# A slot's gathers, a finished tile's root and two exponentials put at other places in the second step of a top-p graph layer

## The chip, the core and the metric

The kernel runs on one core of one Trainium2 chip. A time is the device time of one execution in microseconds. The core has five engines that work side by side, each through its own list of instructions in order: PE (matmuls and transposes), ACT (activation functions and copies out of PSUM), DVE (passes over rows, maxima), POOL (small arithmetic, and the gathers, whose addresses it works out) and SP (which only issues transfers). They wait for one another by semaphores.

## The reference

A graph of N = 3327 nodes with 256 features each. After a layer norm with ReLU, two steps are made; in each, an attention over all nodes is cut to the largest probabilities that make up 0.9 of a row (top-p), and the sparse adjacency matrix spreads the features.

```python
def _top_p_attention(X, W1, W2, W3):
    q = X @ W1.T @ W2.T
    k = X @ W3.T
    probs = jax.nn.softmax(q @ k.T / TAU, axis=-1)
    idx = jnp.argsort(-probs, axis=-1)
    sp = jnp.take_along_axis(probs, idx, axis=-1)
    keep_sorted = jnp.cumsum(sp, axis=-1) - sp < TOP_P
    ...
    A = probs * mask
    return A / jnp.maximum(A.sum(-1, keepdims=True), 1e-12)
...
for n in range(STEPS):
    A = _top_p_attention(Xa, W1, W2, W3)
    Xf = R @ Xf
    Xa = A @ Xa
    Z = Z + Xf @ U1[n].T + Xa @ U2[n].T
h = X + Z
...
x = x + layernorm(h)
```

R is the adjacency plus the identity, each row divided by its sum.

## The kernel before

The nodes stand in 26 tiles of 128 rows. For each tile a row of 3328 exponentials `e` is made, and the top-p threshold of each row is found without sorting: it is guessed from a law of the row's moments, the guess is measured with a few passes over `e`, and then the exact threshold is settled among the candidates just below the guess. The second step runs in slots, one per tile, and a slot holds work of several tiles at once, each at another stage. A slot has seven parts (k = 0 to 6). What stands in a part, and in which order, is written out by hand: `PLAN[1]` has a string per part, and each letter lets one piece of work go one yield further. The lists of PE, ACT, DVE and POOL keep exactly this order (an in-order dependency is put between each two neighbours). Slots -1 to 3 and 25 to 27 have strings of their own (`OPEN`, `LAST`); `PLAN[1]` rules slots 4 to 24.

The letters of slot i, with the lines that matter here:

- `m`, the guess for tile i+1 (`measured_twice`). In k=0 ACT works out the first guess (up to L676) and POOL prepares columns of `g` (L677, L678, L679). In k=1 and 3 ACT makes two passes over `e` (L634). In k=4 DVE takes their sums (L686, L687), ACT a logarithm and an exponential (L688, L689), POOL four operations (L690 to L693). In k=5 comes a third pass (L634). In k=6 DVE, ACT and POOL make the second guess of it (DVE L700, L701, L707, L708; ACT L703 to L705; POOL L698, L699, L709 to L713). `n` in the next slot's k=1 is its last exponential on ACT (L715).
- `d` and `c`, settling tile i (`settle`) on DVE: the pass L730 makes `w`, the values below the guess (k=2); 20 MAX8 (L735) take the best of each segment; L742 and L744 sort out the best 40; the pass L764 masks `e` with the threshold (`c`, next slot's k=0).
- `w`, the exponentials of tile i+2: four quarters, each of matmuls (L601) and an exponential on ACT (L605; the last one L609 and L611); two in k=2, one in k=4, one in k=6. `q` makes the queries of tile i+3 (L524, L529).
- `g`, the gathers of tile i+2 (`refetch`, `fetched`): POOL issues five indirect transfers of 128 rows (L922) into one of two buffers `xg`. Together with the first, SP is asked for the packed adjacency (`ac` from `cx`).
- `s`, the sparse product of tile i from its gathered rows: six matmuls (L930), the result added on DVE (L1120).
- `f`, finishing tile i-2: DVE adds the attention's sum (L954) and takes the statistics (L459, L460); POOL makes the root (L466, L467, L962: the reciprocal standard deviation and its product with the mean); in the next slot's k=2 POOL scales the tile (L969 to L972) and SP sends it out.

Between the letters PE transposes `e` in seven groups (L810), ACT copies each out (L812), and PE multiplies them with the features (L824). In L679, `g`'s column 3 is read, into which L686 writes the next value of that column:

```python
G.tensor_scalar(col(7), col(3), ms(3), ms(8), ALU.mult, ALU.add)
...
V.tensor_scalar(col(3), oa[:, 1:2], float(NP), col(9), ALU.add, ALU.mult)
```

Of the kernel before, what the change touches and what calls it, by code (L numbers as in the profile page):

```python
# [345 lines left out]
def guess_graph_layer(ctx, tc, x, adj, w1t, w2t, w3t, u1t, u2t, ln_g, ln_b, out, flag):  # L346
# [780 lines left out]
    def refetch(t):  # L1127
# [7 lines left out]


    PLAN = (("gmdsssa", "gmcdsssa", "edawwpg", "gmsdga", "gmspdea", "ohgdawwqg", "gehmgq"),
            ("llcmss", "lnms", "lwwnfd", "lcmdsssgggg", "fdsmwqdf", "llmdf", "lmwdg"))

    LAST = {NT - 1: ("cfss", "cn", "nd", "sss", "fddddddsf", "f", ""), NT: ("c", "", "", "ff", "ff", "fv", "f"),  # L1140
            NT + 1: ("fv", "f", "", "", "f", "f", "f")}
# [98 lines left out]
@with_exitstack  # L1240
def tile_graph_layer(ctx, tc, *args):
    keep = ctx.enter_context(tc.tile_pool(name="keep", bufs=1))
    flag = keep.tile([1, 1], I32, tag="flag", name="flag")
    guess_graph_layer(tc, *args, flag)
    failed = tc.nc.values_load(flag[0:1, 0:1], min_val=0, max_val=1 << 20)
    with tc.If(failed > 0):
        search_graph_layer(tc, *args)
# [34 lines left out]
```

## Time and profile before

| | |
|---|---|
| median of three runs | 1345.82 us (1345.72 to 1351.75) |
| the profiled execution | 1354.65 us, its span 1352.9 us |
| second step, from L730 of tile 0 to the end of the span | 771.10 to 1352.9 us |
| busy over the span: PE, DVE, ACT, POOL | 1269.8, 1164.4, 1082.9, 1019.6 us |
| granted TensorE clock over the span | 0.985; 1.00 in all windows from 830 to 1280 us |

Rows of a timeline give start, duration (both in us), engine, line, operation, the tile written and those read, shapes, and how many instructions the row stands for; in brackets stands how long the engine was idle just before, and what ended that. Rows of windows give the stretch, its length, then the busy time of PE, of PE's weight loads, of DVE, ACT and POOL with the number of instructions, and then the granted clock, the transfers' share and GB/s. Matmuls' ends are modelled, and spans on POOL are rough.

### The profile page before, as it was taken

The page shows a single profiled execution, that of the slowest core. Times are in us where ns is not written, and L with a number is a line of the kernel's source. Part 1 is how long each engine was busy: PE and PEld are TensorE (multiplying, and loading weights), DVE is VectorE, ACT ScalarE, POOL GpSimd, SP SyncE. Part 2 cuts the span into 40 slices and gives each one's busy share as a digit, 9 for nine tenths or more (in the row PEclk, how much of TensorE's full clock was granted, in tenths as well). Part 3 has the DMA queues.
Part 4 walks back from the last instruction along what each step waited for, and adds up shares of the span by engine and source line. Part 5 has one row for each costly group of instructions (what it writes and reads, how often), then busy time and mean ns, then how long its engine had stood idle before and what let it go on. Part 6 is the DMA issues. An engine that isn't in the chain of part 4 may idle for free.

```text
span 1352.9 us, 22127 instructions
## 1 busy us (share of the span) xinstructions
PE 1269.8 (94%) x6495; PEld 976.5 (72%) x6495; DVE 1164.4 (86%) x3481; ACT 1082.9 (80%) x2368; POOL 1019.6 (75%) x1405
## 2 busy tenths in 40 slices
PE   5989999999999999999999579999999999999985
PEld 4635777878777777777777457777777777777774
DVE  5867799999999999999890689899898989989893
ACT  4385788888888879888763789999998999999951
POOL 5114788888888888887883577888888888888862
PEclk9999999999999999999999879999999999999998
DMA  8634545454454544545443212221212222131200
GB/s 276 205 127 131 146 137 159 125 151 146 136 158 124 160 139 137 157 133 152 125 111 88 73 53 68 74 90 51 91 56 86 64 82 87 54 90 51 91 24 23
DMA packets 92642, 149.77 MB, mean 111 GB/s; under 512 B 15425, under 2 KB 59072, under 8 KB 92512
## 3 DMA queue, kind: packets, MB, share of 16 engines
q1 hardware_dynamic: 75056, 105.37, 24.5%
q0 software_dynamic: 16640, 42.69, 12.4%
q8 instruction: 54, 0.88, 0.3%
q14 instruction: 76, 0.62, 0.1%
q10 hardware_dynamic: 816, 0.20, 0.1%
HBM read 120.93 MB, written 27.28 MB: 110 GB/s over the span
## 4 chain that ended last, share of the span: by engine, by line
DVE 34%; ACT 25%; PE 21%; POOL 11%; issue 5%; DMA 3%; SPq 0%; another core or an unknown queue 0%; DVEq 0%; POOLq 0%; ACTq 0%
ACT ja L634 13%; PE pa L824 8%; DVE cand L735 7%; DVE w L730 5%; DVE e L764 4%; DVE fm L854 4%; PE pl L601 3%; ACT e L605 2%; ACT eT L812 2%; PE pz L1012 2%; PE pt L810 2%; POOL g L713 2%; DVE cand L744 2%; DVE bb L742 2%; POOL xg L922 2%
## 5 line engine op out<-in xcount | busy, mean ns | idle before, releaser
L824 PE MATMUL pa<-xw,eT 128*128 128x256 f32 x1352 | 322.3, 383 | 4.0 <-DVE s L954 4.0
L634 ACT ACTIVATE ja<-e,g 128x3328 uint8<-128x3328 f32 x106 | 325.7, 3072 | 0.1
L824 PE MATMUL pa<-x,eT 128*128 128x256 f32 x1352 | 322.1, 379 | 0.0
L824 PEld LDWEIGHTS pa<-xw,eT 128*128 128x128 f32 x1352 | 249.9, 190 | 52.7 <-issue 13.8
L824 PEld LDWEIGHTS pa<-x,eT 128*128 128x128 f32 x1352 | 242.8, 190 | 25.8 <-ACT xa L833 0.2
L735 DVE MAX8 cand<-w 128x8 f32<-128x168 f32 (+1 forms) x1040 | 253.4, 319 | 0.0
L901 POOL DMA_INDIRECT ac<-in_adj,index x130 | 202.9, 1561 | 60.2 <-issue 24.4
L812 ACT COPY eT<-pt 128x512 f32<-128x512 f32 (+1 forms) x364 | 199.6, 556 | 43.3 <-PE pt L810 38.7
L922 POOL DMA_INDIRECT xg<-bx,index x130 | 177.2, 1363 | 50.1 <-issue 23.1
L810 PE MATMUL pt<-ident,e 128*128 128x128 f32 x1144 | 176.2, 276 | 18.0 <-DVE e L761 8.6
L810 PEld LDWEIGHTS pt<-ident,e 128*128 128x128 f32 x1144 | 139.7, 144 | 60.1 <-issue 23.6
L730 DVE SCALAR_TENSOR_TENSOR w<-e,g 128x3328 f32<-128x3328 f32 x44 | 166.9, 3793 | 6.4 <-ACT g L715 6.3
L922 POOL DMA_INDIRECT xg<-vx,index x130 | 140.2, 1078 | 34.0 <-issue 29.8
L930 PE MATMUL pr<-xg,ac 128*128 128x257 f32 (+1 forms) x520 | 140.6, 394 | 9.0 <-DVE s L1120 7.3
L764 DVE SCALAR_TENSOR_TENSOR e<-e,rec 128x3328 f32<-128x3328 f32 x40 | 147.2, 3681 | 0.6
L605 ACT ACTIVATE e<-pl 128x832 f32<-128x832 f32 x132 | 113.1, 861 | 31.6 <-PE pl L601 20.7
L930 PEld LDWEIGHTS pr<-xg,ac 128*128 128x128 f32 x520 | 93.7, 194 | 34.5 <-issue 14.0
L601 PE MATMUL pl<-both,qT 64*128 64x416 f32 x416 | 91.8, 539 | 8.3 <-DVE e L1018 3.6
L601 PE MATMUL pl<-after,qT 64*128 64x416 f32 x416 | 95.3, 552 | 1.1 <-ACT e L605 1.1
L854 DVE TENSOR_REDUCE fm<-at 128x4 f32<-128x512 f32 (+1 forms) x133 | 84.5, 635 | 7.0 <-DMA at<-in_adj 5.6
L742 DVE MAX8 bb<-cand 128x8 f32<-128x160 f32 x234 | 75.6, 323 | 4.6
L634 ACT ACTIVATE ja<-x,g 128x3328 uint8<-128x3328 f32 x24 | 73.7, 3072 | 0.0
(260 smaller groups left out, 2132.3 us busy)
## 6 DMA issues: line engine op xcount, KB each, us to landing
at<-in_adj SPq DMA_DIRECT2D x114, 256.0 KB
cx<-ac SPq DMA_DIRECT2D x26, 384.0 KB
ac<-cx SPq DMA_DIRECT2D x26, 384.0 KB
wide<-in_adj SPq DMA_DIRECT2D x8, 832.0 KB
e<-in_adj SPq DMA_DIRECT2D x6, 832.0 KB
own<-bx SPq DMA_DIRECT2D x26, 128.5 KB
x<-in_x SPq DMA_DIRECT2D x13, 256.0 KB
xr<-in_x SPq DMA_DIRECT2D x26, 128.0 KB
```

Source lines behind the costliest of these rows:

```text
L601: PE.matmul(pl[:, a, :wd], qT[p, :], keys_of(step, a).rearrange("p a b -> p (a b)")[:, c : c + wd], start=True, stop=True)
L605: S.activation(e.rearrange("p (a n) -> p a n", a=2)[:, :, c : c + wd], pl[:, :, :wd], AF.Exp, accum_out=za[:, n : n + 1])
L634: S.activation(ja, e, f, bias=guess, scale=sign, accum_out=total)
L730: V.scalar_tensor_tensor(w, e, col(16), e, ALU.is_lt, ALU.mult, accum_out=d2)
L735: V.max(cand[:, 8 * s : 8 * s + 8], w[:, s * SEG : min(NP, (s + 1) * SEG)])
L764: V.scalar_tensor_tensor(e, e, at(1), e, ALU.is_ge, ALU.mult, accum_out=ra)
L810: PE.transpose(pt[:, j, :], e[:, (j0 + j) * P : (j0 + j + 1) * P], ident)
L812: S.copy(eT[:, :w, :], pt[:, :w, :])
L824: PE.matmul(self.pa, eT[:, c - 4 * k, :], self.xa[:, j, :], start=c == 0, stop=c == NT - 1)
L901: G.indirect_dma_start(out=ac[:, k, :], out_offset=None, in_=rows, in_offset=bass.IndirectOffsetOnAxis(ap=index[:, t, k : k + 1], axis=0), ...
L922: G.indirect_dma_start(out=xg[:, k, :w], out_offset=None, in_=rows, in_offset=bass.IndirectOffsetOnAxis(ap=index[:, t, k : k + 1], axis=0))
L930: PE.matmul(pr[:, :w], ac[:, k, :], own if k == KT - 1 else xg[:, k, :w], start=k == 0, stop=k == KT - 1)
```

## The change

One table row of the plan for the second step is written anew. In part 3 four `g` go, in part 6 there are five in a row in place of one; the second `f` after the slot's sum (the root) goes from the end of part 5 to the end of part 6; in parts 4 and 6 `w` stands before `m`.

```diff
     PLAN = (("gmdsssa", "gmcdsssa", "edawwpg", "gmsdga", "gmspdea", "ohgdawwqg", "gehmgq"),
-            ("llcmss", "lnms", "lwwnfd", "lcmdsssgggg", "fdsmwqdf", "llmdf", "lmwdg"))
+            ("llcmss", "lnms", "lwwnfd", "lcmdsss", "fdswmqdf", "llmd", "lwmdgggggf"))
```

PE's, DVE's and SP's lists stay the same, instruction by instruction. POOL's list in the middle of a slot, from the end of the scaling of a finished tile (L971, L972) on, before:

```order
L971 TENSOR_TENSOR xr<-xr,bet 128x256
L972 TENSOR_TENSOR s_10495<-s_10495,xr 128x256
L922 DMA xg<-vx,index 128x256 x4
L690 TENSOR_SCALAR g<-g 128x1
L691 TENSOR_SCALAR g<-g 128x1
L692 TENSOR_SCALAR g<-rec,g 128x1
L693 TENSOR_SCALAR g<-g 128x1
L466 TENSOR_SCALAR rstd<-mv 128x1
L467 TENSOR_TENSOR rstd<-rstd,half 128x1
L962 TENSOR_SCALAR nm<-mv,rstd 128x1
L698 TENSOR_SCALAR g<-oa 128x1
```

The same place now:

```order
L971 TENSOR_TENSOR xr<-xr,bet 128x256
L972 TENSOR_TENSOR s_10495<-s_10495,xr 128x256
L690 TENSOR_SCALAR g<-g 128x1
L691 TENSOR_SCALAR g<-g 128x1
L692 TENSOR_SCALAR g<-rec,g 128x1
L693 TENSOR_SCALAR g<-g 128x1
L698 TENSOR_SCALAR g<-oa 128x1
```

The four gathers (L922) and the three operations of the root (L466, L467, L962) are gone from between the guess's operations.

POOL's list at the slot's end, from the guess's last operation (L713) to the next slot's first columns (L677 to L679) and the scaling of the finished tile (L969), before:

```order
L712 TENSOR_SCALAR g<-g 128x1
L713 TENSOR_TENSOR g<-g 128x1
L922 DMA xg<-vx,index 128x256
L677 TENSOR_SCALAR g<-g,law 128x1
L678 TENSOR_SCALAR g<-g 128x1
L679 TENSOR_SCALAR g<-g,law 128x1
L969 TENSOR_SCALAR s_10495<-s_10495,rstd,nm 128x256
```

The same place now:

```order
L712 TENSOR_SCALAR g<-g 128x1
L713 TENSOR_TENSOR g<-g 128x1
L922 DMA xg<-vx,index 128x256 x5
L466 TENSOR_SCALAR rstd<-mv 128x1
L467 TENSOR_TENSOR rstd<-rstd,half 128x1
L962 TENSOR_SCALAR nm<-mv,rstd 128x1
L677 TENSOR_SCALAR g<-g,law 128x1
L678 TENSOR_SCALAR g<-g 128x1
L679 TENSOR_SCALAR g<-g,law 128x1
L969 TENSOR_SCALAR s_10495<-s_10495,rstd,nm 128x256
```

Five gathers and the root now stand ahead of L677, where one gather stood.

ACT's list in parts 5 and 6 of a slot, as a piece of the difference (`ja` is what a pass over `e` writes and doesn't keep, `oa` its sum, `pl` the logits in PSUM):

```order
 L634 ACTIVATE ja,oa<-e_99,g 128x3328
 L812 COPY eT<-pt 128x512
+L609 ACTIVATE e_100,za<-pl 128x2x415
+L611 ACTIVATE e_100,za<-pl 128x1
 L703 ACTIVATE g<-g,one 128x1
 L704 ACTIVATE g<-g 128x1
 L705 ACTIVATE g<-g,one 128x1
-L609 ACTIVATE e_100,za<-pl 128x2x415
-L611 ACTIVATE e_100,za<-pl 128x1
```

The last quarter's exponential (L609, L611) now stands ahead of the guess's operations of part 6. In the same way the third quarter's (L605) stands ahead of L688 and L689 in part 4, where it stood behind them.

## The prediction

> **What bounds the kernel now.** I read the windows first, one per slot of the second step, from one pass L730 (`w`, the candidates below the guess) to the next.
>
> ```profile
> 1200.52:1221.98 21.46, 21.46 (x114) 17.00 (x113) 19.34 (x58) 19.14 (x40) 18.79 (x27) 1.00 0.25 75
> 1221.98:1243.72 21.74, 20.54 (x106) 15.81 (x105) 19.46 (x57) 21.08 (x40) 17.87 (x28) 1.00 0.25 79
> sum 43.20, PE 42.00 PEld 32.81 DVE 38.80 ACT 40.21 POOL 36.66; mean PE 21.00 PEld 16.41 DVE 19.40 ACT 20.11 POOL 18.33
> ```
>
> In the first of these slots PE has no idle time (21.46 of 21.46 us), in the second 1.2 us; over both it works 42.00 of 43.20 us, 21.00 a slot. ACT works 20.11 a slot, DVE 19.40, POOL 18.33. So PE could hold a slot at about 21.0 us, ACT at about 20.1, and everything is close: any engine that is made to wait becomes the bound. How long a slot is on average comes from the rows L730 of tile 5, tile 6 and tile 24:
>
> ```profile
> 877.65 3.67 DVE L730 SCALAR_TENSOR_TENSOR w<-x,g 128x3328 f32<-128x3328 f32 x1
> 898.68 3.91 DVE L730 SCALAR_TENSOR_TENSOR w<-e,g 128x3328 f32<-128x3328 f32 x1 [0.30 <-ACT g L715]
> 1286.28 3.67 DVE L730 SCALAR_TENSOR_TENSOR w<-e,g 128x3328 f32<-128x3328 f32 x1
> ```
>
> From the first to the last, 19 periods in 408.63 us are 21.51 us each, 0.5 above PE's own work. The rest is made by POOL and DVE. The timelines of both, for the first slot above and the end of the one before it (the L764 at 1302.14 is tile 24's, for later):
>
> ```profile
> 1196.71 3.69 DVE L764 SCALAR_TENSOR_TENSOR e<-e,rec 128x3328 f32<-128x3328 f32 x1
> 1200.52 3.67 DVE L730 SCALAR_TENSOR_TENSOR w<-e,g 128x3328 f32<-128x3328 f32 x1
> 1208.35 0.22 DVE L686 TENSOR_SCALAR g<-oa,g 128x1 f32<-128x1 f32 x1 [0.34 <-ACT ja L634]
> 1213.66 0.31 DVE L744 MATCH_REPLACE8 cand<-bb,cand 128x160 f32<-128x160 f32 x1
> 1214.36 0.27 DVE L700 TENSOR_SCALAR g<-oa,g 128x1 f32<-128x1 f32 x1 [0.39 <-POOL g L693]
> 1217.39 3.69 DVE L764 SCALAR_TENSOR_TENSOR e<-e,rec 128x3328 f32<-128x3328 f32 x1
> 1221.98 3.91 DVE L730 SCALAR_TENSOR_TENSOR w<-e,g 128x3328 f32<-128x3328 f32 x1 [0.69 <-ACT g L715]
> 1302.14 3.69 DVE L764 SCALAR_TENSOR_TENSOR e<-e,rec 128x3328 f32<-128x3328 f32 x1
> ...
> 1195.70 0.24 POOL L711 TENSOR_TENSOR g<-g 128x1 f32<-128x1 f32 x1
> 1196.82 4.57 POOL L922 DMA_INDIRECT xg<-vx,index  x1 [0.17 <-issue]
> 1201.45 2.95 POOL L677 TENSOR_SCALAR g<-g,law 128x1 f32<-128x1 f32 x1
> 1204.47 0.24 POOL L678 TENSOR_SCALAR g<-g 128x1 f32<-128x1 f32 x1
> 1204.79 0.34 POOL L679 TENSOR_SCALAR g<-g,law 128x1 f32<-128x1 f32 x1
> 1209.47 0.96 POOL L922 DMA_INDIRECT xg<-vx,index  x1 [0.30 <-issue]
> 1210.73 0.96 POOL L922 DMA_INDIRECT xg<-vx,index  x1 [0.30 <-issue]
> 1212.99 0.27 POOL L690 TENSOR_SCALAR g<-g 128x1 f32<-128x1 f32 x1
> 1214.37 0.24 POOL L466 TENSOR_SCALAR rstd<-mv 128x1 f32<-128x1 f32 x1
> 1215.73 0.26 POOL L698 TENSOR_SCALAR g<-oa 128x1 f32<-128x1 f32 x1
> 1217.46 3.78 POOL L712 TENSOR_SCALAR g<-g 128x1 f32<-128x1 f32 x1
> ```
>
> Two things are to be seen. First, **POOL stands still while DVE makes a pass over a whole row with two inputs in SBUF** (L764, which masks e, and L730, each 3.7 us). L712, an operation on a single column, takes 3.78 us under L764; L677 takes 2.95 and ends 0.2 us behind L730; a gather (L922) that came 0.11 us behind the start of L764 takes 4.57 us instead of 0.96 and ends at 1201.39, 0.99 us behind L764's end at 1200.40. Only work that began first gets through:
>
> ```profile
> 1153.98 3.69 DVE L764 SCALAR_TENSOR_TENSOR x<-x,rec 128x3328 f32<-128x3328 f32 x1
> 1154.01 1.12 POOL L922 DMA_INDIRECT xg<-vx,index  x1 [0.16 <-issue]
> ```
>
> At 0.03 us behind, the gather takes 1.12 us. The limit thus lies between 0.03 and 0.11 us. Between L764's end and L730's start (0.12 us) one POOL instruction slips in: the locked gather itself, then L677 is held.
>
> Second, the guess has to wait here for POOL: four gathers (1.26 us apart) stand before L690, L690 ends before L700 can start (DVE idles 0.39 us), and the root (L466 to L698, 1.36 us) stands before L698, so that L712 runs into L764, and L713 behind it, on which the next L730 waits through L715, is as late. ACT then idles 1.66 us (L715 below) and DVE 0.69.
>
> **The change, part by part.** *Four gathers leave the place ahead of L690, the root leaves the place ahead of L698.* Taken alone that frees POOL by 4 x 1.26 = 5.0 us and 1.36 us in a stretch where DVE loses 0.39 us and L712 is late. This is what could be gained: at most the 0.5 us between 21.51 and PE's 21.0, a slot.
>
> *Five gathers and the root come between L713 and L677.* The number of instructions stays, and SP's queue keeps its order, with one DMA out of `cx` per tile. The gathers that go out at the end of slot i are those of tile i+2, which PE reads in slot i+2, so their landing has a slot to spare. But behind them on POOL stand the root, then L677, L678 and L679, and **L686 on DVE waits for L679**: it writes column 3, which L679 still has to read. Before, that wait was hidden: L679 ended at 1205.13, L686 started at 1208.35, and what it waited for was always ACT's pass:
>
> ```profile
> L686 DVE TENSOR_SCALAR g<-oa,g x19: 213/214/216, 885.4 to 1273.6; 128x1 f32<-128x1 f32 x19
>   ACT ja L634: 14.1, 19
> ```
>
> Queued behind L686 on DVE are ten of the candidates' MAX8, L700, L764 and the next L730; ACT's L688 and so the fourth pass over e hang on it too.
>
> Now the sum, with L730 at 0. Let one gather start just ahead of L764, a second be held under it, and a third be held under L730. L730 ends at 3.67; the third gather ends 0.98 later, at 4.65 (as 0.99 above); the fourth starts 0.30 behind and the fifth 1.26 behind that, so the fifth ends at 4.95 + 1.26 + 0.96 = 7.17; with 0.03 ahead of it the root takes 1.36, to 8.56; L677 to L679 take about 0.98 by their rows (0.32 from L678 to L679, taken twice, and 0.34), so L679 ends at 9.54 and L686 starts at 9.62, in place of 7.83 here. DVE then needs 5.66 us to L700 (1208.35 to 1214.01, just behind the last MATCH_REPLACE8, where L700 was ready but for POOL), 3.03 to L764, and 3.81 from L764 to L730 (1196.71 to 1200.52). 9.62 + 5.66 + 3.03 + 3.81 = **22.12 us a slot**, above PE's 21.0, so DVE and POOL become the bound and PE waits. This ring closes on itself: L730, gathers, L679, L686, L764, L730.
>
> *The exponentials in front.* ACT's rows around them:
>
> ```profile
> 1208.85 0.39 ACT L688 ACTIVATE g<-g,one 128x1 f32<-128x1 f32 x1
> 1209.62 0.84 ACT L605 ACTIVATE x<-pl 128x832 f32<-128x832 f32 x1
> 1210.46 0.25 ACT L529 COPY qT<-pq 128x128 f32<-128x128 f32 x1
> 1210.61 0.59 ACT L812 COPY eT<-pt 128x512 f32<-128x512 f32 x1
> 1211.08 3.08 ACT L634 ACTIVATE ja<-e,g 128x3328 uint8<-128x3328 f32 x1
> 1214.15 0.59 ACT L812 COPY eT<-pt 128x512 f32<-128x512 f32 x1
> 1214.92 0.39 ACT L703 ACTIVATE g<-g,one 128x1 f32<-128x1 f32 x1 [0.19 <-DVE g L701]
> 1215.60 0.37 ACT L705 ACTIVATE g<-g,one 128x1 f32<-128x1 f32 x1
> 1215.88 0.84 ACT L609 ACTIVATE x<-pl 128x830 f32<-128x830 f32 x1
> 1216.86 0.58 ACT L812 COPY eT<-pt 128x512 f32<-128x512 f32 x1
> 1221.56 0.39 ACT L715 ACTIVATE g<-g 128x1 f32<-128x1 f32 x1 [1.66 <-POOL g L713]
> ```
>
> L605 ahead of L688 and L609, L611 ahead of L703 fill what ACT waits for DVE there: 0.19 us at L703 and a little at L688. In the new ring this is no gain in time, since ACT isn't in it. It costs, though: L609 and L611 put 0.98 us (1215.88 to 1216.86) ahead of L703, on the way to L713 and the first gather. From L686: 0.50 to L688, then 0.77, 0.15 and 0.47 to ACT's pass (at 1211.08, without the exponential of 0.84), 3.07 to the copy, 0.47 for it, 0.98, from L703 to the end of L705 1.05, a hop of some 0.1 (an estimate; such hops take 0.04 to 0.1 in these rows), and from L711 to the gather 1.12: 8.68 us. L764 comes at 5.66 + 3.03 = 8.69. **The first gather and L764 start together**; with a limit of 0.03 to 0.11 us in the gather's favour I take it as through, but this is the weakest point. If it is held, four gathers are left behind L730 and the slot is 1.26 longer, 23.38.
>
> *How many slots.* The plan's line rules slots 4 to 24; gathers run out after tile 25's, so 20 groups are moved (tiles 6 to 25). In the first nothing has shifted yet and the gather is held: 23.38 in place of 21.03. Then 18 slots at 22.12 are 398.2 against 387.6 now (898.68 to 1286.28): +10.6. In the last, L764 comes at 9.62 + 5.66 + 3.03 = 18.31 in place of 15.86 (1286.28 to 1302.14): +2.5. Sum 2.4 + 10.6 + 2.5 = **+15.5 us**. The profiled execution took 1354.65 us (span 1352.9), so 1370.2; the median of the runs shown, 1345.82, lies 8.8 below that execution, and I carry the difference over: 1361.3, given as 1361.
>
> Bounds: the slot's first term would be nothing if L679 came before 7.83 (no change), and the highest is 23.38 a slot, with the gather held.
>
> A rule of the Trainium skill speaks for the other way. In "SBUF — State Buffer", section "Who interferes with whom", it says that a DVE instruction with two SBUF inputs contends only with GpSimd's reads, and that writing descriptors needs the write interface; by that a gather's descriptors could be made all through L764 and L730. The row of 4.57 us differs for a gather that begins behind L764, the one of 1.12 agrees for one already begun. By the rule the second rival below would hold, some 1335.
>
> **The rivals.** (1) *The first gather is held too*, in all slots: 18 slots of 23.38 are 420.8, +33.2, with +2.4 and +3.7 at the ends +39.3: 1385. For it: the tie above, and L711 on ACT's side now 0.98 later. Against: the limit leaves the gather 0.1 us.
>
> (2) *Faster*: POOL gets through the gathers before L730 has begun, or they run on under it. Place: the stretch from L713 to L679. Then only root and L677 to L679 are left, held to L730's end: 3.67 + 0.2 + 1.36 + 0.98 = 6.2, before L686's 7.83; the relief stays, ACT's two waits are filled, and PE bounds with 21.0: 20 x -0.5 is -10, 1335.5. It decides from the point at which no more than one gather is left behind L730 (with one left L679 ends at 7.0). For it: the bound of PE and the waits of 1.66 and 0.69 us that go. Against: five gathers need 6.3 us, and L764 starts about when the first does.
>
> (3) *No change*: the relief ahead of L690 (DVE's 0.39 and 0.69 us, half of the slots) pays for the later L686, as where two gathers are left (L686 at 9.62 - 1.26 = 8.36, and 20.86 a slot by the ring, so that PE's 21.0 and now and then an L713 held under L764 decide again): 1346.
>
> **How the numbers follow.** Forecast 0.42, first rival 0.28, faster 0.13, no change 0.17. About 0.5%, 6.7 us, is what can be told from no change. The forecast and the first rival lie above 1352.5: slower 0.70; same 0.17; faster 0.13. The range goes from 1338, which leaves out most of the faster case, to 1391, above the first rival by the 0.3 us a slot by which my rows differ (L730 takes 3.67 or 3.91): about 0.82 of the chances.
>
> **What would show it.** Right: gathers of over 4 us in the timeline of POOL under L764 and again under L730, DVE idle ahead of L686 in every slot from tile 6 on with POOL's L679 as what ends it, 1.5 to 2 us each (now ACT's pass and 0.7 on average), L700 no longer waiting for POOL, slots near 22.1, and PE idle by over 1 us a slot. Gathers of 1 us inside L764 and L686 at 8 would be the faster case; three long waits and slots of 23.4 the first rival. The forecast is wrong altogether if L686 goes on waiting for ACT.

## The result and the profile after

| | before | after |
|---|---|---|
| median | 1345.78 us (1345.72 to 1351.75, 4 runs) | 1382.06 us (1380.86 to 1382.71, 4 runs) |
| ratio | | 1.0266, 95% interval 1.0243 to 1.0289 |
| the profiled execution, its span | 1354.65, 1352.9 us | 1382.12, 1380.4 us |
| tile 6's L730 to tile 24's, 18 slots | 387.60 us (21.53 each) | 415.07 us (23.06 each) |

The changed kernel is slower by 36.3 us, where +15 was forecast. It is the case of the first rival (1385): the first gather is held too, and four gathers are left behind L730 instead of three. The windows of two slots of the changed kernel, with the columns of before:

```profile
1126.38:1149.43 23.05, 21.27 (x108) 16.29 (x108) 19.09 (x57) 19.91 (x40) 17.93 (x27) 1.00 0.22 69
1149.43:1172.49 23.06, 21.28 (x108) 16.30 (x108) 19.09 (x57) 19.93 (x40) 17.96 (x27) 1.00 0.23 69
```

Every engine now idles: PE, which had no idle time in one slot of two, loses 1.78 us in each, DVE 3.96, ACT 3.1, POOL 5.1. No engine bounds the slot by its work; a ring of waits does. It can be followed in the timelines of POOL and DVE, from one L764 to the L730 behind the next:

```profile
1122.57 3.69 DVE L764 SCALAR_TENSOR_TENSOR e<-e,rec 128x3328 f32<-128x3328 f32 x1
1126.38 3.66 DVE L730 SCALAR_TENSOR_TENSOR w<-x,g 128x3328 f32<-128x3328 f32 x1
1137.04 0.21 DVE L686 TENSOR_SCALAR g<-oa,g 128x1 f32<-128x1 f32 x1 [3.27 <-POOL g L679]
1142.58 0.27 DVE L700 TENSOR_SCALAR g<-oa,g 128x1 f32<-128x1 f32 x1
1145.63 3.69 DVE L764 SCALAR_TENSOR_TENSOR x<-x,rec 128x3328 f32<-128x3328 f32 x1
1149.43 3.67 DVE L730 SCALAR_TENSOR_TENSOR w<-x,g 128x3328 f32<-128x3328 f32 x1
...
1123.35 3.92 POOL L922 DMA_INDIRECT xg<-vx,index  x1 [0.90 <-issue]
1127.57 3.30 POOL L922 DMA_INDIRECT xg<-vx,index  x1 [0.30 <-issue]
1131.17 0.95 POOL L922 DMA_INDIRECT xg<-vx,index  x1 [0.31 <-issue]
1132.42 0.95 POOL L922 DMA_INDIRECT xg<-vx,index  x1 [0.30 <-issue]
1133.67 0.95 POOL L922 DMA_INDIRECT xg<-vx,index  x1 [0.30 <-issue]
1134.70 0.24 POOL L466 TENSOR_SCALAR rstd<-mv 128x1 f32<-128x1 f32 x1
1136.67 0.33 POOL L679 TENSOR_SCALAR g<-g,law 128x1 f32<-128x1 f32 x1
1144.60 0.23 POOL L711 TENSOR_TENSOR g<-g 128x1 f32<-128x1 f32 x1 [0.25 <-ACT g L705]
1145.31 0.19 POOL L713 TENSOR_TENSOR g<-g 128x1 f32<-128x1 f32 x1
1146.09 4.22 POOL L922 DMA_INDIRECT xg<-vx,index  x1 [0.59 <-issue]
```

The first gather starts 0.46 us behind the second L764 here (1146.09 against 1145.63) and takes 4.22 us; the one behind it meets L730 and takes 3.30; three more, the root and L677 to L679 follow, and L679 ends at 1137.00, 10.62 us behind L730. L686 has waited 3.27 us for it. From L686 it is 8.59 us to L764 and 3.80 to L730: 10.66 + 8.59 + 3.80 = 23.05. All instructions of L686's line show the same wait, where ACT's pass stood before:

```profile
L686 DVE TENSOR_SCALAR g<-oa,g x19: 212/214/215, 883.4 to 1298.5; 128x1 f32<-128x1 f32 x19
...
  POOL g L679: 59.4, 19
```

59.4 us over 19 slots are 3.1 us each. What this hands on, in the list of waits between 900 and 1300 us (what waited, for whom, us in total, times, longest):

```profile
ACT g L688 <- DVE g L687: 47.8, 18, 2.8
PEld pt L810 <- ACT qT L529: 30.5, 17, 2.0
```

L700, ahead of which DVE idled 0.39 us before, now starts without a wait. The profiled executions differ by 27.5 us, 27.47 of them between tile 6's L730 and tile 24's; the rest cancels (-2.90 ahead of it, +2.93 behind it). The medians differ by 36.3, because the profiled execution of before lay 8.8 us above its median.

### The profile page after: what moved, and what is told of

Read it like the earlier page. It is cut to its first block, busy times and chain, and to the rows that moved or that the text cites. A ratio compares the mean times of both kernels' runs of the same rounds, so it can differ in the third digit from the quotient of the medians.

```text
span 1380.4 us, 22146 instructions
## 1 busy us (share of the span) xinstructions
PE 1276.8 (92%) x6495; PEld 975.3 (71%) x6495; DVE 1159.1 (84%) x3481; ACT 1080.1 (78%) x2368; POOL 1008.0 (73%) x1405
## 4 chain that ended last, share of the span: by engine, by line
PE 37%; DVE 22%; POOL 22%; ACT 10%; issue 6%; DMA 2%; SPq 0%; POOLq 0%; ACTq 0%; DVEq 0%
PE pa L824 16%; POOL xg L922 15%; DVE cand L735 6%; PE pl L601 5%; ACT ja L634 5%; PE pt L810 4%; PE pr L930 4%; PE pz L943 2%; PE pz L1012 2%; DVE cand L744 2%; DVE w L730 2%; DVE bb L742 2%; DVE e L764 2%; DVE fm L854 2%; PE pk L1056 1%
## 5 line engine op out<-in xcount | busy, mean ns | idle before, releaser
L824 PE MATMUL pa<-xw,eT 128*128 128x256 f32 x1352 | 326.1, 386 | 1.9 <-DVE s L954 1.8
L634 ACT ACTIVATE ja<-e,g 128x3328 uint8<-128x3328 f32 x106 | 325.7, 3073 | 0.1
L922 POOL DMA_INDIRECT xg<-vx,index x130 | 237.0, 1823 | 46.0 <-issue 44.4
L901 POOL DMA_INDIRECT ac<-in_adj,index x130 | 198.6, 1528 | 59.7 <-issue 25.7
L922 POOL DMA_INDIRECT xg<-bx,index x130 | 179.9, 1384 | 50.7 <-issue 21.2
L730 DVE SCALAR_TENSOR_TENSOR w<-e,g 128x3328 f32<-128x3328 f32 x44 | 165.4, 3759 | 2.2 <-ACT g L715 2.1
L764 DVE SCALAR_TENSOR_TENSOR e<-e,rec 128x3328 f32<-128x3328 f32 x40 | 147.2, 3681 | 0.6
L605 ACT ACTIVATE e<-pl 128x832 f32<-128x832 f32 x132 | 113.6, 865 | 30.6 <-PE pl L601 25.1
L634 ACT ACTIVATE ja<-x,g 128x3328 uint8<-128x3328 f32 x24 | 73.7, 3070 | 0.0
```

The source lines that it names most:

```text
L605: S.activation(e.rearrange("p (a n) -> p a n", a=2)[:, :, c : c + wd], pl[:, :, :wd], AF.Exp, accum_out=za[:, n : n + 1])
L634: S.activation(ja, e, f, bias=guess, scale=sign, accum_out=total)
L730: V.scalar_tensor_tensor(w, e, col(16), e, ALU.is_lt, ALU.mult, accum_out=d2)
L764: V.scalar_tensor_tensor(e, e, at(1), e, ALU.is_ge, ALU.mult, accum_out=ra)
L824: PE.matmul(self.pa, eT[:, c - 4 * k, :], self.xa[:, j, :], start=c == 0, stop=c == NT - 1)
L901: G.indirect_dma_start(out=ac[:, k, :], out_offset=None, in_=rows, in_offset=bass.IndirectOffsetOnAxis(ap=index[:, t, k : k + 1], axis=0), ...
```

## The experiments

Each kernel differs from the changed one or from the one before only by what its diff shows (`...` marks the part of a line that is left out), and computes the same. Each was timed beside the kernel before on the same chip, and its ratio is to that; the chip is not the same for all of them. The theory after the result: the slot is the ring L730, gathers behind L730, root, L679, L686, L764, L730; four gathers are left behind L730 because the first starts just behind L764, and each one fewer is worth 1.26 us a slot.

### One part undone at a time

**L686 writes a column of its own**, so that it needn't wait for L679 (`g` is one column wider):

```diff
-        col = guessed(r, small.tile([P, 18], F32, tag="g", name="g"), 1)
+        col = guessed(r, small.tile([P, 19], F32, tag="g", name="g"), 1)
...
-        V.tensor_scalar(col(3), oa[:, 1:2], float(NP), col(9), ALU.add, ALU.mult)
-        V.tensor_scalar(col(4), col(3), 0.5, oa[:, 0:1], ALU.mult, ALU.subtract)
+        V.tensor_scalar(col(18), oa[:, 1:2], float(NP), col(9), ALU.add, ALU.mult)
+        V.tensor_scalar(col(4), col(18), 0.5, oa[:, 0:1], ALU.mult, ALU.subtract)
```

> The changed kernel, but L686 writes a column of its own (19 columns in g), so it no longer waits for L679. Theory (the ring L730, held gathers, root, L679, L686, L764): DVE doesn't wait ahead of L686 any more, only ACT's L689 still needs L679's result (10.62 us behind L730), 0.97 us earlier than it comes now. L764 then starts some 17.9 us behind L730 instead of 19.25: a slot of 21.7 (22.2 if L713 is held under L764) instead of 23.06, 1355 to 1365 us. Rival (POOL's time held under the passes is the bound by itself, whoever waits for it): 1382 as it is. Rival (the exponentials in front cost the time): 1382.

Measured: 1353.91 us (1352.08 to 1355.2), ratio 1.0044 (1.0029 to 1.0058). 28 of the 36 us go with one dependency, though not one instruction of POOL has moved. Timelines of DVE, ACT and POOL:

```profile
1138.98 0.21 DVE L686 TENSOR_SCALAR g<-oa,g 128x1 f32<-128x1 f32 x1
1146.36 0.27 DVE L700 TENSOR_SCALAR g<-oa,g 128x1 f32<-128x1 f32 x1 [1.75 <-POOL g L693]
1149.39 3.70 DVE L764 SCALAR_TENSOR_TENSOR x<-x,rec 128x3328 f32<-128x3328 f32 x1
...
1142.17 0.39 ACT L689 ACTIVATE g<-g 128x1 f32<-128x1 f32 x1 [1.62 <-POOL g L679]
...
1150.20 3.89 POOL L922 DMA_INDIRECT xg<-vx,index  x1 [0.59 <-issue]
```

L686 starts without a wait, and the wait turns up further on: ACT's L689, which also needs L679's result, waits 1.62 us for it, and ACT's pass (L634) and POOL's L693 come behind L689. The pass, with the reading of its sum, and L693 end within 0.02 us of each other, and L700 waits 1.75 us for them (the profile names now one, now the other). The slots are 21.70 us, so the late L679 still costs 0.7 over PE's 21.0. It is POOL's list behind L730 that is late; L686 was the first to feel it.

**The root back ahead of L698:**

```diff
-            (..., "lcmdsss", "fdswmqdf", "llmd", "lwmdgggggf"))
+            (..., "lcmdsss", "fdswmqdf", "llmdf", "lwmdggggg"))
```

> The changed kernel with the root back at the end of part 5, the five gathers still at the slot's end. Theory of the ring: L679 ends 1.36 us earlier (9.26 us behind L730), L686 with it, a slot of 21.7 us, 1355 us. Rival (only the gathers count, the root is hidden): 1380 or so. Rival (POOL's whole work is the bound, and the root only changes its place): 1382.

Measured: 1355.25 us (1354.45 to 1358.46), ratio 1.0056 (1.0035 to 1.0077). L686 waits 2.00 us instead of 3.27 and the slots are 21.76 us, 1.30 less; the root's own 1.36 was to be had. The first gather starts 0.54 behind L764 there, and is held too.

**The exponentials back behind the guess operations**, in both parts:

```diff
-            (..., "lcmdsss", "fdswmqdf", "llmd", "lwmdgggggf"))
+            (..., "lcmdsss", "fdsmwqdf", "llmd", "lmwdgggggf"))
```

> The changed kernel with the exponentials behind the guess's operations again, gathers and root as changed. Theory of the ring: the last pass over e ends 0.84 us later behind L686, so L700 and L764 0.46 later; the first gather would start some 0.2 us behind L764 instead of 0.46. If it is still held, 23.5 us a slot, 1391 us; if it gets through, three gathers are left and the slot is 22.3, 1366. Rival (the exponentials in front hold up the guess and cost the 36 us): 1346.

Measured: 1388.51 us (1387.37 to 1391.57), ratio 1.0305 (1.0285 to 1.0325): the first gather is still held, though it now starts 0.23 us behind L764 instead of 0.46. The timelines of ACT, DVE and POOL say why it got no better:

```profile
1140.10 0.84 ACT L605 ACTIVATE e<-pl 128x832 f32<-128x832 f32 x1
1141.56 3.08 ACT L634 ACTIVATE ja<-x,g 128x3328 uint8<-128x3328 f32 x1
...
1138.83 0.21 DVE L686 TENSOR_SCALAR g<-oa,g 128x1 f32<-128x1 f32 x1 [3.27 <-POOL g L679]
1144.84 0.28 DVE L700 TENSOR_SCALAR g<-oa,g 128x1 f32<-128x1 f32 x1 [0.40 <-ACT ja L634]
1147.87 3.68 DVE L764 SCALAR_TENSOR_TENSOR x<-x,rec 128x3328 f32<-128x3328 f32 x1
...
1147.32 0.19 POOL L713 TENSOR_TENSOR g<-g 128x1 f32<-128x1 f32 x1
1148.10 4.46 POOL L922 DMA_INDIRECT xg<-vx,index  x1 [0.59 <-PE pt L810]
```

L605 stands ahead of the pass L634 again, L700 waits 0.40 us for that pass, and the slot grows to 23.5. So in this ring ACT's order counts, by 0.47 us a slot. L700 starts 6.01 us behind L686 here (1144.84 - 1138.83), as it did before (1214.36 - 1208.35 in the prediction's rows), and 0.20 us behind the end of ACT's pass, also as before, although the four gathers have left the place ahead of L690. L713 now ends 0.36 us ahead of L764, but a tile's first gather has 0.59 us ahead of it in which POOL does nothing; it starts 0.23 behind L764 and takes 4.46 us. That gap became the next suspect.

**The exponentials alone in front, in the kernel before:**

```diff
-            (..., "lcmdsssgggg", "fdsmwqdf", "llmdf", "lmwdg"))
+            (..., "lcmdsssgggg", "fdswmqdf", "llmdf", "lwmdg"))
```

> The kernel before with the exponentials in front of the guess's operations, gathers and root left where they were. Theory: L679 stays early (4 us behind L730), so the ring is not closed; ACT no longer waits for DVE at L688 and L703, but L713 comes later by up to 0.7 us and meets L764 more often: 1339 to 1356. Rival (the exponentials in front cost the 36 us): 1382.

Measured: 1349.32 us (1344.92 to 1353.52), ratio 1.0009 (0.9993 to 1.0025): no difference. The whole loss is that of the gathers and the root. L700 comes 5.7 to 5.8 us behind L686 in this kernel, instead of 6.01, with the four gathers still ahead of L690; one slot in DVE's timeline:

```profile
1119.57 0.21 DVE L686 TENSOR_SCALAR g<-oa,g 128x1 f32<-128x1 f32 x1 [1.20 <-ACT ja L634]
1125.35 0.27 DVE L700 TENSOR_SCALAR g<-oa,g 128x1 f32<-128x1 f32 x1 [0.17 <-ACT ja L634]
```

### The first gather against L764

**The gathers shifted by one.** One gather of slot 3 is left for slot 4. From then on the five behind L713 are a tile's fifth and the next tile's first four; number and place stay.

```diff
-    OPEN[2] = OPEN[3] = OPEN[1]
+    OPEN[2] = OPEN[1]
+    OPEN[3] = OPEN[1][:6] + ("mwd",)
```

> The changed kernel, with one gather of slot 3 left for slot 4, so that from slot 4 on the first gather behind L713 is a tile's fifth and the tile's first comes second. Theory (the first gather is held because it starts 0.46 us behind L764, and that is because a tile's first gather has 0.59 us of issue ahead of it): the gather now starts 0.17 us behind L713, 8.63 behind L686, and L764 at 8.59: within 0.05 us of each other. If it gets through, three gathers are left behind L730 and the slots are 23.06 - 1.26 = 21.8 us, 1382 - 18 x 1.26 = 1359; if it is still held, 23.06 and 1382. A theory by which the gathers' places do not matter, only their number: 1382 and unchanged rows ahead of the first gather (0.59).

Measured: 1363.45 us (1353.62 to 1365.7), ratio 1.012 (1.0085 to 1.0155). Both cases occur in one execution; from the timelines of POOL and DVE:

```profile
1092.45 3.69 DVE L764 SCALAR_TENSOR_TENSOR e<-e,rec 128x3328 f32<-128x3328 f32 x1
1115.51 3.70 DVE L764 SCALAR_TENSOR_TENSOR e<-e,rec 128x3328 f32<-128x3328 f32 x1
...
1092.57 4.57 POOL L922 DMA_INDIRECT xg<-vx,index  x1 [0.17 <-issue]
1115.55 1.12 POOL L922 DMA_INDIRECT xg<-vx,index  x1 [0.17 <-issue]
```

The gap is 0.17 us for a fifth gather behind L713, as the theory had it. 0.12 us behind L764 the gather takes 4.57 us and the next slot is 23.07; 0.04 behind it takes 1.12 and the next slot is 21.77. In this execution six gathers stood at 0.12 and twelve at 0.04.

**The same shift, with the exponentials back**, where L764 comes later:

```diff
-            (..., "lcmdsss", "fdswmqdf", "llmd", "lwmdgggggf"))
+            (..., "lcmdsss", "fdsmwqdf", "llmd", "lmwdgggggf"))
...
-    OPEN[2] = OPEN[3] = OPEN[1]
+    OPEN[2] = OPEN[1]
+    OPEN[3] = OPEN[1][:6] + ("mwd",)
```

> The same shift, with the exponentials back behind the guess operations in both parts (as in the run that took 1388.5 with the first gather 0.23 us behind L764 and held for 4.46). Theory: 0.42 us less ahead of the gather puts it 0.19 us ahead of L764, so it gets through in about 1.1 us; three are left behind L730 and the slots fall from 23.52 to 22.26: 1388.5 - 18 x 1.26 = 1366, which is the prediction's forecast of three left behind L730. Rival (a first gather is held whenever L764 follows it closely, or the issue time is not the tile's first gather's own): still 1388.

Measured: 1363.9 us (1362.95 to 1364.69), ratio 1.0148 (1.0124 to 1.0173), 24.6 us less than the same order without the shift. One slot in the timelines:

```profile
1156.20 1.12 POOL L922 DMA_INDIRECT xg<-vx,index  x1 [0.17 <-issue]
1157.63 3.27 POOL L922 DMA_INDIRECT xg<-vx,index  x1 [0.30 <-issue]
1161.21 3.48 POOL L922 DMA_INDIRECT xg<-vx,index  x1 [0.30 <-issue]
...
1156.40 3.69 DVE L764 SCALAR_TENSOR_TENSOR x<-x,rec 128x3328 f32<-128x3328 f32 x1
1169.62 0.21 DVE L686 TENSOR_SCALAR g<-oa,g 128x1 f32<-128x1 f32 x1 [2.03 <-POOL g L679]
```

The gather starts 0.20 us ahead of L764, in other slots 0.28, and is through in every slot; one gather under L764, one under L730, two more behind it; L686 waits 2.03 us, the slots are 22.26. This is the forecast's own case, three gathers left behind L730: it gave 22.12 a slot and 1361 us. That the two lie so near is in part luck: L686 comes at 9.41 us behind L730 instead of 9.62, and L764 9.05 us behind L686 instead of 8.69. With the exponentials in front, as in the forecast, the slots in which the gather got through were 21.8.

**One gather ahead of L698**, where POOL idled 1.08 us for ACT's pass:

```diff
-            (..., "lcmdsss", "fdswmqdf", "llmd", "lwmdgggggf"))
+            (..., "lcmdsss", "fdswmqdf", "llmd", "lwgmdggggf"))
```

> The changed kernel with one of the five gathers ahead of the last guess operations (ahead of L698, where POOL idles 1.08 us a slot for ACT's pass), four behind L713. Theory: the gather ahead costs L698 some 0.2 us at most; of the four, one is held under L764, one under L730, so L679 ends 1.26 us earlier behind L730 and the slots are 23.06 - 1.26 = 21.8 us: 1359. If the gather behind L713 gets through as well (0.17 us ahead of it instead of 0.59, as not the tile's first), only two are left behind L730, the ring gives 20.5 us, below PE's 21.0, and the time is about 1340. Rival (the cost is the root's and the gathers' total on POOL, or L698's delay passes to L713 and L715): no less than 1375.

Measured: 1339.85 us (1332.51 to 1345.21, 10 runs), ratio 0.9954 (0.9934 to 0.9974): 42 us below the changed kernel and 6 below the one before, by the place of one gather in five. The first gather behind L713 is now a tile's second, so the gap goes as well. Again both cases stand in one execution:

```profile
1076.64 3.69 DVE L764 SCALAR_TENSOR_TENSOR e<-e,rec 128x3328 f32<-128x3328 f32 x1
1097.18 3.69 DVE L764 SCALAR_TENSOR_TENSOR e<-e,rec 128x3328 f32<-128x3328 f32 x1
...
1076.67 1.06 POOL L922 DMA_INDIRECT xg<-vx,index  x1 [0.17 <-issue]
1097.29 4.54 POOL L922 DMA_INDIRECT xg<-vx,index  x1 [0.17 <-issue]
```

At 0.03 us (eleven slots) the next slot is 20.56 us, at 0.11 (six slots) 21.8. The time is that expected with every gather through, 1340, but with a mixture: that case had been reckoned with PE's 21.0 us a slot, and 21.06 is the mean of these slots (tile 6 to tile 24).

### Looking for the rest

**Three gathers where four stood before, one ahead of L698**, the rest as before:

```diff
-            (..., "lcmdsssgggg", "fdsmwqdf", "llmdf", "lmwdg"))
+            (..., "lcmdsssggg", "fdsmwqdf", "llmdfg", "lmwdg"))
```

> A version meant to be faster than both: the order of before, but with three gathers in the fourth part instead of four, and one behind the root in the sixth part, ahead of L698; exponentials as before, one gather at the slot's end. Theory (before, POOL's four gathers behind L679 bring L690 and so L700 late in half of the slots, 0.39 and 0.69 us, and PE waits 0.8 there): L690 comes 1.26 earlier, L700 no longer waits for POOL, the gather ahead of L698 falls into POOL's idle time, and all slots go at PE's 21.0: 20 x 0.37 = 7 us less than before, some 1339. Rival (PE and L713 under L764 bind in the same slots whatever POOL does ahead of L690): 1346.

Measured: 1345.45 us (1339.92 to 1349.96, 12 runs), ratio 1.0004 (0.9989 to 1.0019). The rival holds. The slots come in threes of 20.7, 21.1 and 21.7 us; in one of three L713 is held under L764 (3.40 us), and L715 waits for it; L677 or L678 is held under L730 in each. L690 comes 1.26 us earlier for nothing: L700 still waits 0.39 us and starts 0.2 us behind the end of ACT's pass, 6.01 us behind L686, as before.

**Two gathers ahead of L698; root and one gather ahead of it; and a split into one, one and three:**

```diff
-            (..., "lcmdsss", "fdswmqdf", "llmd", "lwmdgggggf"))
+            (..., "lcmdsss", "fdswmqdf", "llmd", "lwggmdgggf"))
...
+            (..., "lcmdsss", "fdswmqdf", "llmdf", "lwgmdgggg"))
...
+            (..., "lcmdsssg", "fdswmqdf", "llmdf", "lwgmdggg"))
```

> The changed kernel with two of the five gathers ahead of L698, three behind L713. Theory: with one ahead the slots were 20.56 us where the gather behind L713 got through and 21.82 where it was held; with one fewer behind L713 the held slots are 20.56 and PE bounds the others, at about 20.5: some 18 x 0.5 = 9 us less than with one ahead, 1331. The second gather ahead costs POOL 1.25 us ahead of L698, of which 0.8 is idle today ahead of L709 and L711. Rival: it makes L713 late by 0.4 us or more, L713 is held under L764 and L715 comes late: 1340 or more.

> The changed kernel with the root and one gather ahead of L698, in this order, and four gathers behind L713. Theory: L679 then ends 1.36 us earlier behind L730 than with one gather ahead alone, so the slots are PE's 20.5 or, where the gather behind L713 is held, 20.5 as well: 1331. Root and gather together are 2.6 us ahead of L698, as with two gathers ahead. Rival as there: L713 late and held under L764, 1340 or more.

> One gather in the fourth part (behind L679), the root and one gather ahead of L698, three gathers behind L713. Theory: two fewer instructions on the way from L730 to L679 than needed; L690 and L693 come 1.25 us later than with one ahead, which just fits ahead of L700 (ready 5.7 us behind L686): PE bounds at 20.5, 1331. Rival: L700 waits for L693 again, as before the change, 1340.

Measured: 1343.36 us (1337.81 to 1346.81), 1347.53 (1343.67 to 1351.67) and 1344.59 (1342.83 to 1347.67); ratios 0.9987 (0.9973 to 1.0002), 1.0024 (1.0009 to 1.0038) and 1.0004 (0.9993 to 1.0015). All three theories missed, and in the same way, by the rival of the first two. With two ahead, the timelines of DVE, POOL and ACT:

```profile
1143.41 3.69 DVE L764 SCALAR_TENSOR_TENSOR x<-x,rec 128x3328 f32<-128x3328 f32 x1
1147.60 3.68 DVE L730 SCALAR_TENSOR_TENSOR w<-e,g 128x3328 f32<-128x3328 f32 x1 [0.30 <-ACT g L715]
...
1143.54 3.60 POOL L713 TENSOR_TENSOR g<-g 128x1 f32<-128x1 f32 x1
...
1147.17 0.39 ACT L715 ACTIVATE g<-g 128x1 f32<-128x1 f32 x1 [1.93 <-POOL g L713]
```

L713 starts 0.13 us behind L764 and is held for 3.60 us; L715 and so the next L730 wait for it. With the root and a gather ahead it is L712 that is held, 3.67 us. The slots alternate: 20.92 and 21.45 with two ahead, 21.30 and 21.45, 20.97 and 21.45. What was moved ahead of L698 to make L679 early made L713 late; there is room for one gather, not for two.

**One gather ahead of L698, and the last exponential back behind L703 to L705** (part 6 alone; the one in part 4 stays in front):

```diff
-            (..., "lcmdsss", "fdswmqdf", "llmd", "lwmdgggggf"))
+            (..., "lcmdsss", "fdswmqdf", "llmd", "lgmwdggggf"))
```

> The changed kernel with one gather ahead of L698 and, in the slot's last part alone, the exponentials L609 and L611 back behind the guess operations L703 to L705. Theory: with one gather ahead, the gather behind L713 stood 0.03 us behind L764 in the slots of 20.56 us (1.08 long) and 0.11 behind in those of 21.82 (4.53 long); L711 waited 0.25 for ACT's L705, and L705 comes 0.3 earlier without L609 and L611 ahead of L703, so the gather starts 0.2 us ahead of L764 and gets through in every slot: 6 to 7 slots 1.26 shorter, 1340 - 8 = 1332. Rival (L609 and L611, now 0.7 us later, make PE's transposes wait, or L764 moves ahead with L705 and the tie stays): 1340 or more.

Measured: **1334.22 us** (1333.81 to 1337.23), ratio 0.9924 (0.9905 to 0.9943): below both kernels, by 0.8% and 3.5%. POOL and DVE in a timeline, then the windows of two slots:

```profile
1177.58 1.08 POOL L922 DMA_INDIRECT xg<-vx,index  x1 [0.17 <-issue]
...
1167.03 0.48 DVE L954 SCALAR_TENSOR_TENSOR s<-pa,ra,s 128x256 f32<-128x256 f32 x1 [1.10 <-PE pa L824]
1177.79 3.69 DVE L764 SCALAR_TENSOR_TENSOR e<-e,rec 128x3328 f32<-128x3328 f32 x1
...
1057.00:1077.54 20.54, 20.54 (x108) 16.15 (x108) 19.17 (x57) 19.92 (x40) 17.50 (x27) 1.00 0.28 77
1160.73:1181.59 20.86, 20.86 (x110) 16.44 (x109) 19.07 (x57) 20.02 (x40) 17.50 (x27) 1.00 0.26 76
```

The gather stands 0.21 us ahead of L764 and gets through, in all slots but one. PE has no idle time in these two slots, and DVE's L954 waits 1.10 us for PE: the kernel has reached the bound that the prediction named, PE's own work (20.84 us a slot on average from tile 6 to tile 24). Against the kernel with one gather ahead alone the gain is less sure: the intervals of the two ratios, 0.9934 to 0.9974 and 0.9905 to 0.9943, overlap.

## Why the prediction was wrong in its size

**What bounds the kernel, and the ring.** Right in the main. POOL stands still under L764 and L730; L686 waits for L679 by the column; the ring closes as it was written. Removing the dependency took 28 us away, putting the root back 27.

**L700's wait** was read wrongly. The prediction put DVE's 0.39 us ahead of it down to POOL's four gathers. In its own rows, ACT's pass L634 ends at 1214.16 (1211.08 + 3.08) and L700 starts 0.20 us later. In that profile L700 stands 6.01 or 6.02 us behind L686 and 0.2 behind the end of that pass in 18 of the 19 slots that begin with the L730 of tiles 4 to 22 (the other is tile 11's, the longest), while L693 ends anywhere from 0.06 to 0.84 us ahead of it. So it waited for ACT, whose pass stood behind the exponential L605. With the gathers gone and L605 in its old place the 6.01 us stay (the run of 1388.51); with one gather fewer they stay too (1345.45); with L605 in front and all four gathers in place they fall to 5.7 or 5.8 (1349.32). Moving the four gathers away relieved nothing there, and the sum's 5.66 us from L686 to L700, which measured 5.54, was near only because the same change moved L605.

**The step that failed** is the tie: "The first gather and L764 start together; with a limit of 0.03 to 0.11 us in the gather's favour I take it as through". Measured from L686, L711 starts at 7.56 us (1144.60 - 1137.04), to the hundredth what the sum in the prediction had ahead of its last term. That last term, "from L711 to the gather 1.12", measured 1.49 (1146.09 - 1144.60): the row it was taken from was a gather with 0.17 us ahead of it, and a tile's first gather, which the change puts there, has 0.59. L764 came at 8.59 instead of 8.69. So the gather is 0.46 us behind, not at the tie, and is held: four gathers are left behind L730, and a slot takes 23.06 us instead of 22.12. Shifting the gathers by one gives 0.17 back and puts the gather 0.04 to 0.12 behind; with 0.2 us in hand the slots are 22.26 us and the time 1363.9, near the forecast's 22.12 and 1361. The gap was taken from the one gather that stood behind L713 before, a tile's fifth. Before, a tile's first gather stood behind L972, also with a short gap (0.16); none stood behind L713, so the term was unknown, and its bounds belonged into the tie.

**The rival's price.** 23.38 us a slot was worked out, 23.06 measured; of the 0.32 the way to L686 makes 0.22 (10.66 behind L730, against 9.62 + 1.26 = 10.88, mostly since the gather held under L730 ends 0.83 us behind it and not 0.98), L764's 0.10 the rest. By profiled executions the rival was +39.3 and is +27.5; that its 1385 lies so near 1382 is in part luck, since I took off the 8.8 us by which that execution of before lay above its median. Of these 8.8 us, 3.3 lie ahead of the second step (771.10 against 767.83 us in the two executions); where the rest lies stays open, as there is one profile of before.

**The exponentials.** "In the new ring this is no gain in time, since ACT isn't in it" was wrong. The one in part 4, where it stands behind the guess operations, delays the pass that L700 and L698 wait for, and with both exponentials back 6 us are lost (1388.5 against 1382.1). The price of the one in part 6, ahead of L703, was right in kind; it matters where the gather stands at the limit. With one gather ahead of L698, putting L609 and L611 back took the held gathers from six slots to one in the profiled executions; the times, 1339.85 against 1334.22, are of two chips, and the intervals of their ratios overlap.

**The rule on two SBUF inputs.** By the prediction's reading of the Trainium skill, "SBUF — State Buffer", section "Who interferes with whom", a gather's descriptors could be made all through L764 and L730. Gathers of 4.22 and 3.30 us, behind their starts, speak against that reading. The same section also says that such an instruction contends with a GpSimd instruction that reads SBUF. A gather begun 0.03 us behind L764 takes 1.06 us with DVE's pass running on top of it, and the pass takes 3.69 us there as it does where the gather is held. So it seems to be what a gather does first, perhaps the reading of its list of indices, that is held, and not the rest. No run tests this.

## What to carry to other kernels

Work put behind a slot's end is paid where the next slot's first instructions queue behind it; add up all that stands on the engine between the last instruction of one slot and the first that another engine waits for. Where a sum ends in a tie between two starts, no number of it can be taken from a row of a similar instruction in another place (here a gather with another number within its tile); forecast both sides and move the work until it is clear of the tie. Before an idle time is put down to the engine that one row names, see which distance stays the same in all slots (here the 0.20 us from ACT's pass to L700, while L693's varied). A tie may show itself in the times: executions of the two kernels in which the gather behind L713 stood 0.02 to 0.13 us behind L764 differ by 12 and 13 us, those of the changed kernel and of the last one by 2 and 3. It is a hint only: those of the kernel with three gathers in the fourth part differ by 10.

## What the runs showed of the hardware

- **The limit is sharp.** In the second step of the 14 profiled executions, from tile 0's L730 on, 166 gathers began between 0.30 us ahead of the start of an L764 or L730 and 0.05 us behind it: all took 1.06 to 1.14 us. 441 began 0.11 us behind it or later, while it ran: all ended 0.80 to 1.01 us behind the pass's end. None began between 0.05 and 0.11 us.
- **The gap ahead of a tile's first gather depends on what stands ahead of it:** 0.59 us behind L713 (0.90 in one slot of the changed kernel), 0.49 behind L962 (root and one gather ahead of L698), but 0.15 behind L693 and 0.16 behind L972; a fifth or second gather has 0.17 behind L713. In the program the first gather waits for four semaphores (three queues and PE), the others for one or none. That these are taken one after another, and hidden where POOL has longer work ahead, would fit; no run tests it.
- **A one-column operation is held as a gather is**: L713 of 0.19 us took 3.60 when it began 0.13 us behind L764, where a gather of 0.95 us took 4.57 (begun 0.12 behind).
- PE's slots without any idle time were 20.54 us in some places and 20.86 in others of one execution (the windows of the last kernel), at a granted clock of 1.00. Why they differ stays open.
